# A four-layer network on one core: the step size dt as ln(1 + exp(x)), one half of the channels per round, without a lent PSUM bank and with fewer zero matmuls

## The chip, the cores and the metric

The kernel runs on one core of a Trainium2 chip. The time is the device time of that core in microseconds, the median of several runs. The profile is one execution of the program, taken on the chip. The engines are called TensorE (PE in the profile), VectorE (DVE), ScalarE (ACT) and GpSimd (POOL); SyncE (SP) issues the transfers.

## The reference

The network has four layers on four images of 56 x 56 tokens with 96 channels. Layers 2 and 3 are attention without a softmax and a quantised feed-forward part. Layers 0 and 1 each hold a selective scan over four orders of the tokens, and the scan takes most of the time. Cut to what matters:

```python
def selective_ssm(dtw, dtb, xw, A_log, D, seq):      # seq: images, 3136 tokens, 192 channels
    xz = jnp.einsum('bld,kd->blk', seq, xw)
    dt_raw, b_ssm, c_ssm = ...                       # 12 or 6, 16 and 16 columns of xz
    dt = jax.nn.softplus(jnp.einsum('blr,dr->bld', dt_raw, dtw) + dtb)
    a = -jnp.exp(A_log)
    d_a = jnp.exp(dt[..., None] * a)                 # the decays
    d_b = dt[..., None] * b_ssm[:, :, None, :]
    def step(h, inp):
        da_t, db_t, x_t, c_t = inp
        h = da_t * h + db_t * x_t[..., None]         # 192 x 16 states
        y_t = jnp.einsum('bds,bs->bd', h, c_t)
        return (h, y_t)
    ...
    return ys + seq * D
```

The softplus of x is ln(1 + exp(x)).

## The kernel before

The scan is cut into chunks of 448 tokens: 2 layers, 4 images, 4 orders and 7 chunks make 224. A chunk has 8 rounds, r = 0 to 7: two halves of 96 channels (e) times four groups of states (q). A round works on three tiles (g) of 128 rows by 448 tokens. For each, ScalarE makes the decay exp(dt * a) into one PSUM tile `da`, which the next round uses again; VectorE (or GpSimd for one of the three) multiplies dt * u with the B of the states, which TensorE has spread over the rows into one PSUM bank `b`; VectorE scans; GpSimd multiplies the states with C (`hc`); TensorE adds up over the states into the bank `y`, two rounds later, and after the fourth group ScalarE copies the sums to `Y`. While a chunk is scanned, the step sizes dt of the next are prepared. Beside the scan run lanes of side work, the other parts of the network for other images; they share two PSUM banks `ps` and are let in by an estimate of what ScalarE and TensorE have left.

Constants of the pacing:

```python
SPARE = (1.2, 3.0)
ACT_LIMIT, PE_LIMIT = 4.3, 6.0
SOFTPLUS = 2
BANKS, LATE_BANKS = 2, 4
DEPTH, LATE_DEPTH = 3, 6


WARM, FILL, PER_P = 1.9, 0.19, 0.58
```

The step sizes: the matmul for one half of the channels, the one made ahead in a lent bank, and the Softplus of both halves:

```python
    def step_sizes(self, ch):

        nc = self.nc
        ch.cd = self.dram.tile([2 * NS, CS], F32, tag="cd", name="cd", bufs=3)
        nc.sync.dma_start(ch.cd, ch.cf[: 2 * NS])
        ch.pd = [self.step_size(ch, 0, self.pp())]

    def step_size(self, ch, e, ps):
        rows = slice(32, 32 + RANK[ch.l])
        self.nc.tensor.matmul(ps[:C], ch.par.wt[rows, C * e : C * e + C], ch.cf[rows], start=True, stop=True)
        return ps[:C]

    def step_size_ahead(self, ch):

        if self.held < BANKS:
            ch.pd.append(self.step_size(ch, 1, self.ps()[:, :CS]))

    def softplus(self, ch):
        for e in range(NE):
            if e == len(ch.pd):
                ch.pd.append(self.step_size(ch, e, self.pp()))
            dt = self.sp.tile([C, CS], F32, name="dtc")
            self.nc.scalar.activation(dt, ch.pd[e], AF.Softplus, bias=ch.par.dtb[:, e : e + 1])
            ch.dtc.append(dt)
```

What is done for the following chunk in each round r of this one:

```python
        elif r == 1:
            self.step_sizes(follow)
            self.split(follow, 0)
        elif r == 2:
            self.softplus(follow)
            self.split(follow, 1)
        elif r == 3:
            self.times_u(follow, 0)
            for e in range(NE):
                self.park(follow.dtd, follow.dtc[e])
        elif r == 4:
            self.times_u(follow, 1)
            self.park(follow.dud, follow.duc[0])
            self.spread(follow.dt, follow.dtd[0], "dt")
        elif r == 5:
            self.park(follow.dud, follow.duc[1])
            self.spread(follow.du, follow.dud[0], "du")
        if r > 4:
            self.fetch(follow, r - 5)
```

The decay, and the loop over rounds (`begin` makes the spread of B on TensorE and, in most rounds, one of the three products on GpSimd; the yields let the side work, called lanes, put in its instructions):

```python
        def decay(n, g):

            ch, e, q = rounds[n]
            nc.scalar.activation(da[g][:, TOKENS], ch.dt[e][:, g], AF.Exp, scale=ch.par.na[:, e, q, g : g + 1])
# ... cut ...
            b, v, ahead = nxt
            for g in range(2 if ahead else 3):
                nc.vector.tensor_tensor(v[:, g, TOKENS], ch.du[e][:, g], b, ALU.mult)
            self.prepare(ch, nexts.get(ch), r)
            self.half_round()
            self.spend((0.6, 0, 3.8, 0, 0, 0, 0, 0)[r], (0, 1.3, 0, 0, 0, 0, 1.3, 1.3)[r] + 1.3 * (r % NQ == 2))
            self.limit = ACT_LIMIT if r >= SOFTPLUS else 0.5 + 0.95 * 2 * (SOFTPLUS - r)
            yield "C", n, r
            more = n + 1 < len(rounds)
            if more:
                nxt = begin(n + 1)
            ended = None
            if len(late) == 2:
                ended = late.pop(0)
                self.add_up(*ended)
            self.prepare_ahead(afters.get(ch), r)
            for g in range(NG):
                if g == 2:
                    self.half_round()
                    if ended and ended[2] == NQ - 1:
                        self.spend(0.6, 0)
                        self.keep_sums(*ended[:3])
                    if r < SOFTPLUS:
                        self.limit -= 0.95
                    yield "F", n, r
                    if r == 1 and ch in nexts:
                        self.step_size_ahead(nexts[ch])
                nc.vector.tensor_tensor_scan(
                    v[:, g, way], da[g][:, way], v[:, g, way], 0.0, ALU.mult, ALU.add
                )
                if g == 2 and ch.step < NCS - 1:
                    nc.scalar.copy(ch.par.carry[:, e, q].unsqueeze(2), v[:, :, end : end + 1])
                if more:
                    decay(n + 1, g)
                    if g == 0:
                        carried(n + 1, nxt[1])
            hc = sp.tile([128, NG, CS], F32, name="hc", bufs=3)
            nc.gpsimd.tensor_tensor(hc, v[:, :, TOKENS], ch.cb[q][:, 0].unsqueeze(1).to_broadcast([128, NG, CS]), ALU.mult)
            late.append((ch, e, q, hc))
```

Adding up, with its zero matmuls, and the copy of the sums:

```python
        for _ in range(int(max(0.0, WARM - self.work) / FILL + 0.5)):
            nc.tensor.matmul(self.y[:C], self.zeros, self.some, start=False, stop=False)
        self.work = 0.0

        for n, g in enumerate((0, 1, 2, 2)):
            nc.tensor.matmul(
                self.y[32 * n : 32 * n + 32], self.four, hc[:, g], start=n == 3, stop=n == 3 or q == NQ - 1,
            )

    def keep_sums(self, ch, e, q):

        y = self.in_order(self.Y[e], ch.orient, ch.c * CS, CS)
        self.nc.scalar.copy(y, self.y[:C].rearrange("p (a b) -> p a b", b=HS))
```

How a part of the side work is let in: its place names a slot and the banks it holds, and what it costs ScalarE (a) and TensorE (p):

```python
                held = sum(h[2] for h in self.live) - g[2] + new
                fits = held <= self.banks - self.lend or new <= g[2] and held <= self.banks
                if place[0] == self.slot and fits and self.room(act, pe):
                    self.spend(act, pe)
                    g[1], g[2] = next(g[0], None), new
# ... cut ...
    def spend(self, act, pe):
        self.work += PER_P * pe
        self.backlog = [a + b for a, b in zip(self.backlog, (act, pe))]

    def half_round(self):

        self.backlog = [max(0.0, a - b) for a, b in zip(self.backlog, SPARE)]

    def room(self, act, pe):

        a, p = self.backlog
        return not self.paced or (act == 0 or a + act <= self.limit) and (pe == 0 or p + pe <= PE_LIMIT)
```

The call:

```python
        for slot, n, r in net.scans():
            p, u = divmod(n, rounds)
            net.slot, net.lend, net.paced = slot, int(r < 2), True
```

The engines take their instructions in the order of the program. In `spend` the pacing counts what a part will cost; `half_round` takes off what an engine has spare in half a round; `room` refuses a part over the limit.

Of the kernel before, what the change touches and what calls it, by code (L numbers as in the profile page):

```python
# [11 lines left out]
F32 = mybir.dt.float32  # L12
# [8 lines left out]
HS = 56  # L21
L = HS * HS
C = 96
DI = 192
NS = 16
NE = 2
# [16 lines left out]
ACT_LIMIT, PE_LIMIT = 4.3, 6.0  # L43
SOFTPLUS = 2
BANKS, LATE_BANKS = 2, 4
# [118 lines left out]
class Net:  # L164
    def __init__(self, ctx, tc, aps, at, out):
# [5 lines left out]
        self.dram = pool("dram", bufs=1, space=bass.MemoryType.DRAM)  # L171
        self.nw, self.depth, self.banks, self.ring = NW, DEPTH, BANKS, None
        self.setup()
        self.dg = None
        self.kept = (0, 0, 0)
        self.ready = set()
        self.held, self.lend, self.live, self.g = 0, 0, [], {}
        self.backlog, self.limit, self.paced = [0.0, 0.0], ACT_LIMIT, False
        self.work = 0.0
# [10 lines left out]
    def late(self):  # L190

        self.scan_pool.close()
        self.wp = self.pool("late", bufs=2)
        self.nw, self.depth, self.banks = LATE_NW, LATE_DEPTH, LATE_BANKS
        tags = (("ps", BANKS), ("da0", 1), ("da1", 1), ("da2", 1), ("pp", 1), ("b", 1), ("y", 1))
        self.ring = cycle([t for t in tags for _ in range(t[1])])
# [284 lines left out]

    def step_size_ahead(self, ch):

        if self.held < BANKS:
            ch.pd.append(self.step_size(ch, 1, self.ps()[:, :CS]))

    def softplus(self, ch):
        for e in range(NE):
            if e == len(ch.pd):
                ch.pd.append(self.step_size(ch, e, self.pp()))  # L490
            dt = self.sp.tile([C, CS], F32, name="dtc")
            self.nc.scalar.activation(dt, ch.pd[e], AF.Softplus, bias=ch.par.dtb[:, e : e + 1])  # L492
            ch.dtc.append(dt)

# [31 lines left out]
    def prepare(self, ch, follow, r):  # L526
# [7 lines left out]
        if r == 0:  # L534
            self.rows(follow)
        elif r == 1:
            self.step_sizes(follow)
            self.split(follow, 0)
        elif r == 2:
            self.softplus(follow)  # L540
            self.split(follow, 1)
        elif r == 3:
            self.times_u(follow, 0)
            for e in range(NE):
                self.park(follow.dtd, follow.dtc[e])
        elif r == 4:
            self.times_u(follow, 1)
            self.park(follow.dud, follow.duc[0])
            self.spread(follow.dt, follow.dtd[0], "dt")
        elif r == 5:  # L550
            self.park(follow.dud, follow.duc[1])
            self.spread(follow.du, follow.dud[0], "du")
# [31 lines left out]
    def scans(self):  # L584
# [23 lines left out]
        first, second = chunks[:2]  # L608
        self.held = 0
        self.parameters(first)  # L610
# [3 lines left out]
        for r in range(8):  # L614
            self.prepare(Step(), first, r) if r else self.rows(first)
        self.parameters(second)
        self.project_step(second, 0)
# [34 lines left out]
        for n, (ch, e, q) in enumerate(rounds):  # L652
# [8 lines left out]
            self.half_round()  # L661
            self.spend((0.6, 0, 3.8, 0, 0, 0, 0, 0)[r], (0, 1.3, 0, 0, 0, 0, 1.3, 1.3)[r] + 1.3 * (r % NQ == 2))
            self.limit = ACT_LIMIT if r >= SOFTPLUS else 0.5 + 0.95 * 2 * (SOFTPLUS - r)
            yield "C", n, r
# [8 lines left out]
# [3 lines that stand above are left out]
                    if ended and ended[2] == NQ - 1:  # L676
                        self.spend(0.6, 0)
                        self.keep_sums(*ended[:3])
                    if r < SOFTPLUS:
                        self.limit -= 0.95  # L680
                    yield "F", n, r
                    if r == 1 and ch in nexts:
                        self.step_size_ahead(nexts[ch])
                nc.vector.tensor_tensor_scan(  # L684
# [16 lines left out]
    def add_up(self, ch, e, q, hc):  # L701

        nc = self.nc
        if q == 0:
# [3 lines left out]
            nc.tensor.matmul(o, w, self.in_order(a, ch.orient, ch.c * CS, CS), start=True, stop=False)  # L708
        for _ in range(int(max(0.0, WARM - self.work) / FILL + 0.5)):
            nc.tensor.matmul(self.y[:C], self.zeros, self.some, start=False, stop=False)  # L710
# [137 lines left out]
    def window(self, d, rows, c):  # L848

        lo, hi = max(0, CR * c - 1), min(HS, CR * c + CR + 1)  # L850
        t = self.wp.tile([128, CR + 2, HS], F32, name="win", bufs=NWIN)[:rows]
        self.nc.sync.dma_start(
# [4 lines left out]
    def overlap(self, part, n, depth=9, ready=lambda c: True):  # L857
# [5 lines left out]
        while live or c < n:  # L863
# [4 lines left out]
            for g in list(live):  # L868
# [4 lines left out]
                held = sum(h[2] for h in self.live) - g[2] + new  # L873
                fits = held <= self.banks - self.lend or new <= g[2] and held <= self.banks
                if place[0] == self.slot and fits and self.room(act, pe):
                    self.spend(act, pe)
                    g[1], g[2] = next(g[0], None), new
                    if g[1] is None:
                        live.remove(g)
                        self.live.remove(g)  # L880
            self.held = sum(h[2] for h in self.live)
            yield
# [9 lines left out]
    def room(self, act, pe):  # L892

        a, p = self.backlog
        return not self.paced or (act == 0 or a + act <= self.limit) and (pe == 0 or p + pe <= PE_LIMIT)

# [334 lines left out]
def tile_net(ctx: ExitStack, tc: tile.TileContext, aps, at, out):  # L1231
# [5 lines left out]
    def alone(lanes):  # L1237
        net.slot, net.lend, net.paced = "C", 0, False
        while lanes:
# [11 lines left out]
    with tc.manual_schedule(engines={E.PE, E.Activation, E.DVE, E.Pool}):  # L1251
        lanes = []
        for slot, n, r in net.scans():
            p, u = divmod(n, rounds)
            net.slot, net.lend, net.paced = slot, int(r < 2), True
            if slot == "C" and u == 2 and p < 8:
# [29 lines left out]
```

## Time and profile before

| | |
|---|---|
| time, median of 3 runs | 9214.4 us (9179.29 to 9226.93) |
| span of the profiled execution | 9209.2 us |
| mean granted clock of TensorE | 0.887 of full |
| from the first scan on (before: setup) | 111.4 us |
| end of the last scan (after: a tail of side work) | 8836.3 us |
| busy in the loop of scans, TensorE, VectorE, ScalarE, GpSimd | 7480.0, 7809.6, 5945.8, 7759.8 us |
| table loads on ScalarE in the program | 776 |
| zero matmuls | 7084 |

The page lists groups of instructions by line of the kernel, engine, operation and tiles (out<-in), with their count, busy time, the mean of one in ns, and after the bar the idle time of the engine just before them with what ended it. A line of the waits reads: who waited, for whom, us in total, times, longest. A line of the timeline reads: start in us, duration, engine, line, operation, tiles, count, and in brackets idle time before it and what ended that. L684 is the scan, L659 VectorE's products, L631 the decays, L646 and L688 the copies of the state carried from chunk to chunk, L492 the Softplus, L569 the spread of B, L694 the product with C, L710 the zero matmuls, L714 the adding up, L721 the copy of the sums, L479 the matmul of the step sizes.

### The profile page before, as it was taken

What the parts mean: (1) busy time and instruction counts of PE and PEld (TensorE: products, weight loads), DVE (VectorE), ACT (ScalarE), POOL (GpSimd) and SP (SyncE); (2) the same over time, 40 slices, a digit from 0 to 9 for tenths busy, and PEclk for the clock granted to TensorE, in tenths of its full rate; (3) what the DMA queues carried; (4) which work ended last, traced back from release to release, by engine and by line L of the source; (5) the groups of instructions that cost most, each with busy time, mean ns of one, the idle gap of its engine ahead of it and who ended that gap; (6) DMA issues with size and microseconds to landing.
All of it is one profiled execution on the core that took longest, in us unless ns stands there. A gap on an engine that the chain in (4) does not pass through costs nothing. (4 is left out here: it accounts for less than half of the span.)

```text
span 9209.2 us, 124390 instructions
## 1 busy us (share of the span) xinstructions
PE 7868.1 (85%) x35426; PEld 3036.5 (33%) x35426; DVE 7881.9 (86%) x10198; ACT 6148.3 (67%) x12259; POOL 7838.3 (85%) x4320
## 2 busy tenths in 40 slices
PE   7888888898888888988889888887888888987897
PEld 3333333333333333333333333333333333333344
DVE  5999999899998999989988997899888898888941
ACT  5777677676777677766776655577656776566645
POOL 5998989989898989889888997899888998888941
PEclk9899989989899988999888998888888888887986
DMA  5776676667666676767666775566755567655721
GB/s 151 176 179 169 166 171 164 157 153 177 162 168 157 157 181 161 169 150 177 162 148 152 168 170 136 136 153 160 171 138 143 141 164 172 147 138 134 168 77 39
DMA packets 951352, 1418.11 MB, mean 154 GB/s; under 512 B 176578, under 2 KB 943812, under 8 KB 949796
## 3 DMA queue, kind: packets, MB, share of 16 engines
q1 hardware_dynamic: 949888, 1408.37, 63.5%
q8 instruction: 278, 4.55, 0.2%
q14 instruction: 414, 3.39, 0.1%
q10 hardware_dynamic: 772, 1.80, 0.1%
HBM read 1141.42 MB, written 268.14 MB: 153 GB/s over the span
## 5 line engine op out<-in xcount | busy, mean ns | idle before, releaser
L684 DVE TENSOR_TENSOR_SCAN v<-da,v 128x449 f32<-128x449 f32 (+1 forms) x5376 | 5484.4, 1072 | 244.6 <-ACT da L631 111.0
L694 POOL TENSOR_TENSOR hc<-v,cb 128x1344 f32<-128x1344 f32 x1792 | 5168.0, 2885 | 573.5 <-DVE v L684 257.2
L631 ACT ACTIVATE da<-dt,na 128x448 f32<-128x448 f32 x5376 | 3392.8, 635 | 1690.3 <-DVE v L684 1650.9
L659 DVE TENSOR_TENSOR v<-du,b 128x448 f32<-128x448 f32 x4172 | 2342.3, 609 | 663.0 <-PE b L569 532.4
L714 PE MATMUL y<-hc,four 128*32 128x448 f32 x14336 | 1913.8, 609 | 0.0
L710 PE MATMUL y<-w,zeros 128*96 128x448 bf16 x7084 | 1716.6, 380 | 0.0
L639 POOL TENSOR_TENSOR v<-du,cb 128x448 f32<-128x448 f32 x1204 | 1373.7, 1141 | 79.0 <-DMA cb<-cd 41.6
L710 PEld LDWEIGHTS <-zeros 128*96 128x96 bf16 x7084 | 918.5, 130 | 1049.4 <-issue 639.9
L569 PE MATMUL b<-cf,sel 128*128 128x448 bf16 x1792 | 708.3, 395 | 350.9 <-DVE v L659 350.1
L761 POOL TENSOR_TENSOR rs<-rs,power 112x4 f32<-112x4 f32 x252 | 254.2, 1010 | 546.9 <-ACT rs L760 361.6
L427 PE MATMUL pp<-U,wd 96*128 96x448 f32 x896 | 674.5, 840 | 14.3 <-DMA U<-u 14.3
L721 ACT COPY Y<-y 96x448 f32<-96x448 f32 x448 | 341.3, 762 | 468.8 <-PE y L714 468.4
L841 PE MATMUL ps<-win,dg 64*64 64x220 f32 (+10 forms) x1962 | 568.4, 491 | 55.3 <-ACT dtc L492 47.0
L714 PEld LDWEIGHTS y<-hc,four 128*32 128x32 f32 x14336 | 295.3, 113 | 951.0 <-issue 649.1
L498 POOL TENSOR_TENSOR duc<-dtc,U 96x448 f32<-96x448 f32 x448 | 559.6, 1249 | 2.5 <-ACT dtc L492 2.5
L708 PE MATMUL y<-Y,ident 96*96 96x448 f32 x672 | 543.4, 898 | 11.4 <-ACT carry L688 8.9
L631 ACT ACT_TABLE_LOAD x385 | 494.0, 1283 | 15.1 <-DMA dt<-dd 8.3
L582 POOL TENSOR_TENSOR cf<-cf 64x448 f32<-64x448 f32 x448 | 417.7, 932 | 38.1 <-ACT cf L466 3.0
L569 PEld LDWEIGHTS <-sel 128*128 128x128 bf16 x1792 | 195.4, 109 | 741.4 <-issue 737.9
L688 ACT COPY carry<-v 128x3 f32<-128x3 f32 x1536 | 295.7, 193 | 172.1 <-DVE v L684 169.6
L765 PE MATMUL ps<-ident,rs 112*96 112x112 f32 x1752 | 267.7, 308 | 158.3 <-POOL rs L761 87.7
L841 PEld LDWEIGHTS ps<-win,dg 64*64 64x64 f32 (+2 forms) x1962 | 236.8, 169 | 423.7 <-issue 317.2
(414 smaller groups left out, 6457.5 us busy)
## 6 DMA issues: line engine op xcount, KB each, us to landing
cb<-cd SPq DMA_DIRECT2D x3584, 112.0 KB, 4.1
dt<-dd SPq DMA_DIRECT2D x1792, 168.0 KB, 4.4
du<-dd SPq DMA_DIRECT2D x1792, 168.0 KB, 4.2
dd<-dtc SPq DMA_DIRECT2D x448, 168.0 KB, 2.0
dd<-duc SPq DMA_DIRECT2D x448, 168.0 KB, 2.0
U<-u SPq DMA_DIRECT2D x112, 168.0 KB, 4.5
z<-w SPq DMA_DIRECT2D x56, 224.0 KB, 3.8
u<-w SPq DMA_DIRECT2D x56, 224.0 KB, 3.2
```

The costliest lines, as they stand in the source:

```text
L427: self.nc.tensor.matmul(ch.ps.rearrange("p (a b) -> p a b", b=HS), ch.par.wx[:, e], self.in_order(self.U[e], ch.orient, ch.c * CS, CS), st ...
L498: self.nc.gpsimd.tensor_tensor(du.rearrange("p (a b) -> p a b", b=HS), ch.dtc[e].rearrange("p (a b) -> p a b", b=HS), self.in_order(self.U ...
L569: self.nc.tensor.matmul(ps, self.sel[:, q], self.upper(ch.cf), start=True, stop=True)
L631: nc.scalar.activation(da[g][:, TOKENS], ch.dt[e][:, g], AF.Exp, scale=ch.par.na[:, e, q, g : g + 1])
L639: nc.gpsimd.tensor_tensor(v[:, 2, TOKENS], ch.du[e][:, 2], ch.cb[q][:, 1], ALU.mult)
L659: nc.vector.tensor_tensor(v[:, g, TOKENS], ch.du[e][:, g], b, ALU.mult)
L684: nc.vector.tensor_tensor_scan(v[:, g, way], da[g][:, way], v[:, g, way], 0.0, ALU.mult, ALU.add)
L694: nc.gpsimd.tensor_tensor(hc, v[:, :, TOKENS], ch.cb[q][:, 0].unsqueeze(1).to_broadcast([128, NG, CS]), ALU.mult)
L708: nc.tensor.matmul(o, w, self.in_order(a, ch.orient, ch.c * CS, CS), start=True, stop=False)
L710: nc.tensor.matmul(self.y[:C], self.zeros, self.some, start=False, stop=False)
L714: nc.tensor.matmul(self.y[32 * n : 32 * n + 32], self.four, hc[:, g], start=n == 3, stop=n == 3 or q == NQ - 1,)
L841: self.nc.tensor.matmul(o[:, a - r0 : e - r0, x0:x1], diag[:, tap], win[:, a + dy - lo : e + dy - lo, x0 + dx : x1 + dx], start=n == 0, st ...
```

## The change

It writes softplus as two activations, Exp and then Ln of it plus one, so that ScalarE may do it with the tables that the decays use. It does one half of the channels in round 2 and the other in round 3, so that the second half needs no bank of its own: its matmul goes to `pp` after the first half has been read, and the `ps` bank that was lent to it stays with the side work. The limit that held side work back on ScalarE ahead of the Softplus goes; each of the two rounds is charged 1.3 us. The zero matmuls, which keep TensorE at work before an adding up, are left out where the sums are copied right after it. In the part after the scans, windows get as many buffers as there are parts under way (6 for 3). All of it is here:

```diff
--- before.py
+++ after.py
@@ -41,7 +41,6 @@
 
 SPARE = (1.2, 3.0)
 ACT_LIMIT, PE_LIMIT = 4.3, 6.0
-SOFTPLUS = 2
 BANKS, LATE_BANKS = 2, 4
 DEPTH, LATE_DEPTH = 3, 6
 
@@ -169,13 +168,13 @@
         self.big = pool("big", bufs=1)
         self.psum = pool("psum", bufs=1, space=bass.MemoryType.PSUM)
         self.dram = pool("dram", bufs=1, space=bass.MemoryType.DRAM)
-        self.nw, self.depth, self.banks, self.ring = NW, DEPTH, BANKS, None
+        self.nw, self.nwin, self.depth, self.banks, self.ring = NW, NWIN, DEPTH, BANKS, None
         self.setup()
         self.dg = None
         self.kept = (0, 0, 0)
         self.ready = set()
-        self.held, self.lend, self.live, self.g = 0, 0, [], {}
-        self.backlog, self.limit, self.paced = [0.0, 0.0], ACT_LIMIT, False
+        self.live, self.g = [], {}
+        self.backlog, self.paced = [0.0, 0.0], False
         self.work = 0.0
         self.U = [self.big.tile([C, L], F32, name=f"U{e}") for e in range(NE)]
         self.Y = [self.big.tile([C, L], F32, name=f"Y{e}") for e in range(NE)]
@@ -191,7 +190,7 @@
 
         self.scan_pool.close()
         self.wp = self.pool("late", bufs=2)
-        self.nw, self.depth, self.banks = LATE_NW, LATE_DEPTH, LATE_BANKS
+        self.nw, self.nwin, self.depth, self.banks = LATE_NW, LATE_DEPTH, LATE_DEPTH, LATE_BANKS
         tags = (("ps", BANKS), ("da0", 1), ("da1", 1), ("da2", 1), ("pp", 1), ("b", 1), ("y", 1))
         self.ring = cycle([t for t in tags for _ in range(t[1])])
 
@@ -479,18 +478,15 @@
         self.nc.tensor.matmul(ps[:C], ch.par.wt[rows, C * e : C * e + C], ch.cf[rows], start=True, stop=True)
         return ps[:C]
 
-    def step_size_ahead(self, ch):
-
-        if self.held < BANKS:
-            ch.pd.append(self.step_size(ch, 1, self.ps()[:, :CS]))
-
-    def softplus(self, ch):
-        for e in range(NE):
-            if e == len(ch.pd):
-                ch.pd.append(self.step_size(ch, e, self.pp()))
-            dt = self.sp.tile([C, CS], F32, name="dtc")
-            self.nc.scalar.activation(dt, ch.pd[e], AF.Softplus, bias=ch.par.dtb[:, e : e + 1])
-            ch.dtc.append(dt)
+    def softplus(self, ch, e):
+
+
+
+
+        dt = self.sp.tile([C, CS], F32, name="dtc")
+        self.nc.scalar.activation(dt, ch.pd[e], AF.Exp, bias=ch.par.dtb[:, e : e + 1])
+        self.nc.scalar.activation(dt, dt, AF.Ln, bias=1.0)
+        ch.dtc.append(dt)
 
     def times_u(self, ch, e):
 
@@ -537,14 +533,15 @@
             self.step_sizes(follow)
             self.split(follow, 0)
         elif r == 2:
-            self.softplus(follow)
+            self.softplus(follow, 0)
             self.split(follow, 1)
         elif r == 3:
+            self.softplus(follow, 1)
             self.times_u(follow, 0)
-            for e in range(NE):
-                self.park(follow.dtd, follow.dtc[e])
+            self.park(follow.dtd, follow.dtc[0])
         elif r == 4:
             self.times_u(follow, 1)
+            self.park(follow.dtd, follow.dtc[1])
             self.park(follow.dud, follow.duc[0])
             self.spread(follow.dt, follow.dtd[0], "dt")
         elif r == 5:
@@ -606,13 +603,14 @@
                             setattr(ch, n_, [])
                         chunks.append(ch)
         first, second = chunks[:2]
-        self.held = 0
         self.parameters(first)
         self.inputs(first)
         self.project_step(first, 0)
         self.project_step(first, 1)
         for r in range(8):
             self.prepare(Step(), first, r) if r else self.rows(first)
+            if r == 2:
+                first.pd.append(self.step_size(first, 1, self.pp()))
         self.parameters(second)
         self.project_step(second, 0)
         self.project_step(second, 1)
@@ -659,8 +657,7 @@
                 nc.vector.tensor_tensor(v[:, g, TOKENS], ch.du[e][:, g], b, ALU.mult)
             self.prepare(ch, nexts.get(ch), r)
             self.half_round()
-            self.spend((0.6, 0, 3.8, 0, 0, 0, 0, 0)[r], (0, 1.3, 0, 0, 0, 0, 1.3, 1.3)[r] + 1.3 * (r % NQ == 2))
-            self.limit = ACT_LIMIT if r >= SOFTPLUS else 0.5 + 0.95 * 2 * (SOFTPLUS - r)
+            self.spend((0.7, 0, 1.3, 1.3, 0, 0, 0, 0)[r], (0, 1.3, 1.3, 0, 0, 0, 1.3, 1.3)[r] + 1.3 * (r % NQ == 2))
             yield "C", n, r
             more = n + 1 < len(rounds)
             if more:
@@ -676,11 +673,9 @@
                     if ended and ended[2] == NQ - 1:
                         self.spend(0.6, 0)
                         self.keep_sums(*ended[:3])
-                    if r < SOFTPLUS:
-                        self.limit -= 0.95
                     yield "F", n, r
-                    if r == 1 and ch in nexts:
-                        self.step_size_ahead(nexts[ch])
+                    if r == 2 and ch in nexts:
+                        nexts[ch].pd.append(self.step_size(nexts[ch], 1, self.pp()))
                 nc.vector.tensor_tensor_scan(
                     v[:, g, way], da[g][:, way], v[:, g, way], 0.0, ALU.mult, ALU.add
                 )
@@ -706,7 +701,7 @@
             o = self.y[:C].rearrange("p (a b) -> p a b", b=HS)
             a, w = (self.U[e], self.skip[ch.l][:, e]) if ch.skip else (self.Y[e], self.ident[:C, :C])
             nc.tensor.matmul(o, w, self.in_order(a, ch.orient, ch.c * CS, CS), start=True, stop=False)
-        for _ in range(int(max(0.0, WARM - self.work) / FILL + 0.5)):
+        for _ in range(int(max(0.0, WARM - self.work) / FILL + 0.5) if q < NQ - 1 else 0):
             nc.tensor.matmul(self.y[:C], self.zeros, self.some, start=False, stop=False)
         self.work = 0.0
 
@@ -848,7 +843,7 @@
     def window(self, d, rows, c):
 
         lo, hi = max(0, CR * c - 1), min(HS, CR * c + CR + 1)
-        t = self.wp.tile([128, CR + 2, HS], F32, name="win", bufs=NWIN)[:rows]
+        t = self.wp.tile([128, CR + 2, HS], F32, name="win", bufs=self.nwin)[:rows]
         self.nc.sync.dma_start(
             t[:, : hi - lo].rearrange("p a b -> p (a b)"), d[:, lo * HS : hi * HS]
         )
@@ -871,14 +866,12 @@
                 times = {t[0]: float(t[1:]) for t in times}
                 act, pe = times.get("a", 0.0), times.get("p", 0.0)
                 held = sum(h[2] for h in self.live) - g[2] + new
-                fits = held <= self.banks - self.lend or new <= g[2] and held <= self.banks
-                if place[0] == self.slot and fits and self.room(act, pe):
+                if place[0] == self.slot and held <= self.banks and self.room(act, pe):
                     self.spend(act, pe)
                     g[1], g[2] = next(g[0], None), new
                     if g[1] is None:
                         live.remove(g)
                         self.live.remove(g)
-            self.held = sum(h[2] for h in self.live)
             yield
 
     def spend(self, act, pe):
@@ -892,7 +885,7 @@
     def room(self, act, pe):
 
         a, p = self.backlog
-        return not self.paced or (act == 0 or a + act <= self.limit) and (pe == 0 or p + pe <= PE_LIMIT)
+        return not self.paced or (act == 0 or a + act <= ACT_LIMIT) and (pe == 0 or p + pe <= PE_LIMIT)
 
 
     def load(self, i):
@@ -1235,7 +1228,7 @@
         return [lane for lane in lanes if next(lane, lane) is not lane]
 
     def alone(lanes):
-        net.slot, net.lend, net.paced = "C", 0, False
+        net.slot, net.paced = "C", False
         while lanes:
             lanes = go_on(lanes)
             net.slot = "CF"[net.slot == "C"]
@@ -1252,7 +1245,7 @@
         lanes = []
         for slot, n, r in net.scans():
             p, u = divmod(n, rounds)
-            net.slot, net.lend, net.paced = slot, int(r < 2), True
+            net.slot, net.paced = slot, True
             if slot == "C" and u == 2 and p < 8:
 
                 assert p > 5 or not lanes
```

## The prediction

> **What bounds the kernel now.** I read the page's busy times first, then the groups, the waits, and last a timeline of one chunk. The loop of scans runs from 111.4 to 8836.3 us (starts and ends of L684 in the trace), 95% of the span, so its 224 chunks of 8 rounds are what counts.
>
> ```profile
> PE 7868.1 (85%) x35426; PEld 3036.5 (33%) x35426; DVE 7881.9 (86%) x10198; ACT 6148.3 (67%) x12259; POOL 7838.3 (85%) x4320
> ```
>
> Three engines are near 85%, none at 100%. By its busy time VectorE is the first: its scans and products have to be done in any case. So the question is what ends its idle time. From the groups and the waits:
>
> ```profile
> L684 DVE TENSOR_TENSOR_SCAN v<-da,v 128x449 f32<-128x449 f32 (+1 forms) x5376 | 5484.4, 1072 | 244.6 <-ACT da L631 111.0
> L659 DVE TENSOR_TENSOR v<-du,b 128x448 f32<-128x448 f32 x4172 | 2342.3, 609 | 663.0 <-PE b L569 532.4
> ACT da L631 <- DVE v L684: 1650.9, 2126, 6.3
> DVE v L659 <- PE b L569: 532.4, 369, 6.5
> ACT Y L721 <- PE y L714: 468.4, 337, 9.2
> DVE v L684 <- ACT da L631: 111.0, 118, 2.5
>   PEld ps L841: 62.5, 21
>   PE ps L765: 54.7, 22
> ```
>
> ScalarE waits 1651 us for scans, VectorE only 111 us for decays: today ScalarE runs ahead. VectorE's largest wait is for TensorE's spread of B (`b`), 532 us. The last two lines are from the answer on L492, of who waited for the step sizes `dtc`: side work that needs a `ps` bank waits until the Softplus has read the one lent to it, and TensorE, which takes its matmuls in order, keeps `b` back meanwhile.
>
> I then sorted VectorE's idle time by round r of the chunk (each scan triple is one round). A chunk takes 38.96 us, 4.08 of it idle; before round 3 alone it is 1.57, of which 1.24 is the wait for `b`. 49 chunks have no side work (under 0.7 us of ScalarE outside the scan's own lines): 35.8 us each, idle before round 3 0.94, all of it ScalarE's. The 175 others: 39.8 us, idle before round 3 1.75, 1.59 of it for `b`. A quiet chunk, ScalarE and then VectorE around rounds 2 to 4:
>
> ```profile
> 4114.09 1.00 ACT L721 COPY Y<-y 96x448 f32<-96x448 f32 x1 [1.00 <-PE y L714]
> 4114.94 0.63 ACT L631 ACTIVATE da<-dt,na 128x448 f32<-128x448 f32 x1
> 4115.60 1.28 ACT L492 ACT_TABLE_LOAD   x1
> 4116.89 0.63 ACT L492 ACTIVATE dtc<-pp,wd 96x448 f32<-96x448 f32 x1
> 4117.42 0.62 ACT L492 ACTIVATE dtc<-ps,wd 96x448 f32<-96x448 f32 x1
> 4118.06 1.28 ACT L631 ACT_TABLE_LOAD   x1
> 4119.35 0.64 ACT L631 ACTIVATE da<-dt,na 128x448 f32<-128x448 f32 x1
> 4125.81 0.64 ACT L631 ACTIVATE da<-dt,na 128x448 f32<-128x448 f32 x1 [1.84 <-DVE v L684]
> 4129.82 0.64 ACT L631 ACTIVATE da<-dt,na 128x448 f32<-128x448 f32 x1 [1.31 <-DVE v L684]
> 4117.32 1.65 DVE L659 TENSOR_TENSOR v<-du,b 128x448 f32<-128x448 f32 x3
> 4120.14 3.06 DVE L684 TENSOR_TENSOR_SCAN v<-da,v 128x449 f32<-128x449 f32 x3 [1.16 <-ACT v L646]
> ```
>
> The Softplus block runs from 4115.60 to 4119.35, 3.75 us, of which 2.57 are two table loads; VectorE's scans of round 3 stall 1.16 us behind it.
>
> **The arithmetic of a block.** In undisturbed rounds a decay ends 2.3 us before its scan starts (medians of the trace), 2.8 us where VectorE makes three products, as before rounds 3 and 4. That is the slack. Ahead of a round's first decay ScalarE idles 1.31 us (after two products) or 1.84 us (after three), as the brackets above show. So a block of B us makes the decays B minus that idle late, plus what was late already, and VectorE stalls by the lateness over the slack. Tried on the chunk above: the copy of `Y` had made round 2's last decay 1.4 late; 3.75 + 1.4 - 1.31 = 3.84, less 2.8 gives 1.04 against 1.16 seen.
>
> [...]
>
> **The change, part by part.**
>
> 1. **Softplus becomes Exp and Ln.** The text means to save both loads. I choose to doubt that. [...] Nothing in the changed kernel names another set. Then each Ln needs a load, and unless that load fetches the joint set, the next decay needs one back. Two halves, two Ln: 4 loads a chunk where there were 2. Each half then is 0.63 (Exp) + 1.28 + 0.63 (Ln) + 1.28 = 3.82 us, with joints 3.85: a Softplus block of the old length, twice, in rounds 2 and 3. On ScalarE: 224 x about 3.9 = 870 us more busy, to about 7000. I give the joint set one chance in ten.
>
> 2. **No bank lent.** The second step size goes to `pp` after the first Exp has read it. TensorE's waits for `dtc` (about 480 us in the ten largest of that answer, TensorE and its weight loads) should nearly go, and with them most of the 1.59 before round 3 in busy chunks: I take 1.3 off. Side work may hold both banks in rounds 0 and 1.
>
> 3. **The pacing.** Side work on ScalarE was held back over rounds 0 and 1 to make room; now it is not, and rounds 2 and 3 are charged 1.3 us each for what I expect to be 3.85. Busy chunks have 6.7 us of side work on ScalarE, 0.83 a round, and now it also falls into these rounds.
>
> 4. **No zeros ahead of the sums that are copied at once.** The trace has 5.1 zero matmuls ahead of an add-up with q=3 of the first half and 3.6 of the second, some 1950 of 7084; at 0.21 us from one to the next about 410 us of TensorE. TensorE isn't the bound there, but the `Y` copy waits for these sums (468 us), and it stands ahead of decays. In the quiet chunk six zeros took 1.35 us just ahead. So the decay after the copy should be 0.5 late, not 1.4.
>
> Sum for a **quiet** chunk: round 3: late 3.85 + 0.5 - 1.31 = 3.04, stall 0.3. Behind a stall the first decay is late by the slack, and each further one gains about 0.35, as a scan takes 1.02 and a decay with its copies less; so the third is about 2.1 late. Round 4: 2.1 + 3.85 - 1.84 = 4.1, stall 1.3, with the carry's copy 1.45. Together 1.75, against 1.2 now: +0.5, times 49 is +25 us.
>
> A **busy** chunk: with 0.83 of side work in each: round 3 stalls 1.2, round 4 2.1 + 0.83 + 3.85 - 1.84 = 4.94, so 2.2. Together 3.4. Off go 1.3 (the wait for `b`), 0.4 (other idle before round 4, 0.56 now, which hides under the stall) and 0.15 (the ScalarE stall of now before round 3): +1.55, times 175 is +271 us.
>
> Credits: the stall before round 6 behind the `Y` copy, 0.30 in busy chunks, nearly goes: -44. Side work that moves in rounds 0 and 1: I estimate -40. The tail of 373 us gets six window buffers for three: at most -5. Sum 9214 + 25 + 271 - 89 = about **9420 us**.
>
> **The rivals.** (a) The joint set is loaded[...]: no load but side work's, each half 1.26 us, no stall in rounds 3 and 4. Then 1.2 is saved in quiet and about 1.75 in busy chunks: 49 x 1.2 + 175 x 1.75 + 89 = 454, so near 8760 us. For it speaks the name of the change[...]. (b) Four loads, but the bound is the bank: side work in the small rounds is little (0.51, 0.07 and 0.32 us in rounds 0 to 2 now) and stays so; the stalls are those of quiet chunks and freeing the bank pays for them: near 9150. (c) TensorE takes the place of the bank: side work's `ps` tiles now wait for evictions that stand behind two blocks in ScalarE's queue, `b` comes late at rounds 3 and 4 both, and 0.8 us more a busy chunk: near 9560. (d) Fewer zeros lower the granted clock. The zeros' share of TensorE falls by 410 us only, and other matmuls stand next to them; I give it 30 us at most.
>
> **The range.** (a) has 0.1. For four loads my sum lies between (b) and (c), and its largest term, the two stalls in busy chunks, is uncertain by some 1 us a chunk or 175 us. So 9190 to 9650 should hold it 8 times in 10. The lines at 2% are 9030 and 9399: faster 0.10, same 0.35, slower 0.55.
>
> **What would show it.** Table loads: 776 now, about 1220 with four a chunk, about 330 with the joint set. VectorE's wait for decays and carries rises from some 180 us to 500 or more, and stands before rounds 3 and 4; its wait for `b` falls by 200 or more; waits of TensorE for `dtc` nearly vanish; the wait of the `Y` copy falls by about half. I am wrong if the loads don't rise, if the wait for `b` stays, or if the stalls before round 4 are under 1 us.

## The result, and the profile after

The changed kernel takes 9510 us (9484 to 9522, four runs) where the kernel before takes 9211 in the runs beside it: 1.0325 times as long, 95% interval 1.0289 to 1.0361. Every ratio below is likewise against runs of the kernel before that were taken beside it (medians of 9198 to 9211 us). The page of the changed kernel: first busy times, then groups (after the bar the idle time ahead of the group and what ended most of it).

```profile
PE 7874.2 (83%) x33219; PEld 2896.8 (30%) x33219; DVE 7906.5 (83%) x10198; ACT 6929.2 (73%) x13156; POOL 7834.7 (82%) x4320
...
L679 DVE TENSOR_TENSOR_SCAN v<-da,v 128x449 f32<-128x449 f32 (+1 forms) x5376 | 5485.6, 1072 | 538.4 <-ACT v L644 346.9
...
L657 DVE TENSOR_TENSOR v<-du,b 128x448 f32<-128x448 f32 x4172 | 2341.0, 608 | 682.5 <-PE b L566 554.1
...
L629 ACT ACT_TABLE_LOAD x608 | 780.1, 1283 | 19.2 <-DMA dt<-dd 8.5
...
L488 ACT ACT_TABLE_LOAD x448 | 574.8, 1283 | 7.9
```

The loads of the kernel before at the decays (L631) and at the Softplus (L492):

```profile
L631 ACT ACT_TABLE_LOAD x385 | 494.0, 1283 | 15.1 <-DMA dt<-dd 8.3
...
L492 ACT ACT_TABLE_LOAD x224 | 287.4, 1283 | 4.0
```

Of the waits, first four of the changed kernel and then the one of the kernel before for the copy of the carry, L646:

```profile
DVE v L657 <- PE b L566: 554.1, 393, 5.9
...
DVE v L679 <- ACT v L644: 346.9, 327, 3.4
...
ACT Y L716 <- PE y L709: 310.6, 192, 5.3
...
DVE v L679 <- ACT da L629: 133.2, 142, 3.3
```

```profile
DVE v L684 <- ACT v L646: 70.2, 75, 2.6
```

The lines have moved: L679 is the scan, L657 the products, L629 the decays, L487 the Exp and L488 the Ln of the step size, L644 and L683 the copies of the carry, L566 the spread of B, L709 the adding up, L716 the copy of the sums. VectorE does the same work (scans 5486 us, 5484 before) and waits longer: for decays and carries 480 us (346.9 and 133.2), where it was 181 (111.0 and 70.2). ScalarE has 781 us more to do: 449 more table loads (1225, 776 before) at 1283 ns are 576 us of it. Every one of the 448 Ln has a load ahead of it, and L629, the decays, has 608 for 385. So Exp and Ln did not share their tables.

A quiet chunk of the changed kernel, from the load behind the Ln of round 2 to the decay behind the Ln of round 3, and VectorE beside it (start, duration, engine, line, operation; in brackets idle time and what ended it):

```profile
3275.77 1.28 ACT L629 ACT_TABLE_LOAD   x1
3277.07 0.64 ACT L629 ACTIVATE da<-dt,na 128x448 f32<-128x448 f32 x1
...
3278.95 0.62 ACT L487 ACTIVATE dtc<-pp,wd 96x448 f32<-96x448 f32 x1
3279.59 1.28 ACT L488 ACT_TABLE_LOAD   x1
3280.88 0.58 ACT L488 ACTIVATE dtc<-dtc 96x448 f32<-96x448 f32 x1
3281.47 1.28 ACT L629 ACT_TABLE_LOAD   x1
3282.77 0.64 ACT L629 ACTIVATE da<-dt,na 128x448 f32<-128x448 f32 x1
```

```profile
3277.86 3.06 DVE L679 TENSOR_TENSOR_SCAN v<-da,v 128x449 f32<-128x449 f32 x3 [0.74 <-ACT v L644]
3280.83 1.66 DVE L657 TENSOR_TENSOR v<-du,b 128x448 f32<-128x448 f32 x3
3283.56 3.06 DVE L679 TENSOR_TENSOR_SCAN v<-da,v 128x449 f32<-128x449 f32 x3 [1.07 <-ACT v L644]
```

The block of round 3, from its Exp to the next decay, runs from 3278.95 to 3282.77, 3.82 us. VectorE stalls in two rounds, 0.74 and 1.07 us, where in the quiet chunk shown of the kernel before it stalled 1.16 in one.

All kernels side by side, VectorE's idle time ahead of each round, in us per chunk, summed from each run's trace (the mean of 224 chunks). The times are medians; the trace of "both Ln in round 3" is of an execution of 9211 us:

| kernel | 0 | 1 | 2 | 3 | 4 | 5 | 6 | 7 | sum | time |
|---|---|---|---|---|---|---|---|---|---|---|
| before | 0.59 | 0.30 | 0.24 | 1.57 | 0.44 | 0.28 | 0.43 | 0.23 | 4.08 | 9211 |
| after | 0.72 | 0.60 | 0.52 | 0.83 | 1.54 | 0.76 | 0.32 | 0.17 | 5.46 | 9510 |
| joint set | 0.87 | 0.59 | 0.58 | 0.15 | 0.42 | 0.30 | 0.26 | 0.17 | 3.34 | 8981 |
| joint set, one bank in rounds 0, 1 | 0.73 | 0.33 | 0.26 | 0.20 | 0.60 | 0.31 | 0.29 | 0.19 | 2.91 | 8916 |
| before with the joint set | 0.58 | 0.26 | 0.33 | 0.71 | 0.55 | 0.26 | 0.60 | 0.26 | 3.55 | 9078 |
| both Ln in round 3 | 0.80 | 0.61 | 0.35 | 0.15 | 1.39 | 0.29 | 0.28 | 0.25 | 4.12 | 9239 |
| second half in round 4 | 0.60 | 0.64 | 0.57 | 0.89 | 0.68 | 0.41 | 0.52 | 0.30 | 4.61 | 9322 |

The table says where the 299 us are: rounds 3 to 5, where the blocks are, went from 2.29 to 3.13, and rounds 0 to 2 from 1.13 to 1.84. In the two profiled executions the loop of scans takes 334 us more (9059 for 8725) and the tail behind it 29 less (344 for 373).

### The profile page after: what moved, and what is told of

Its sections match the earlier page's. It is cut to its first block, busy times and chain, and to the rows that moved or that the text cites. A ratio compares the mean times of both kernels' runs of the same rounds, so it can differ in the third digit from the quotient of the medians.

```text
span 9517.1 us, 120632 instructions
## 1 busy us (share of the span) xinstructions
PE 7874.2 (83%) x33219; PEld 2896.8 (30%) x33219; DVE 7906.5 (83%) x10198; ACT 6929.2 (73%) x13156; POOL 7834.7 (82%) x4320
## 5 line engine op out<-in xcount | busy, mean ns | idle before, releaser
L679 DVE TENSOR_TENSOR_SCAN v<-da,v 128x449 f32<-128x449 f32 (+1 forms) x5376 | 5485.6, 1072 | 538.4 <-ACT v L644 346.9
L629 ACT ACTIVATE da<-dt,na 128x448 f32<-128x448 f32 x5376 | 3386.3, 635 | 1262.1 <-DVE v L679 1202.0
L657 DVE TENSOR_TENSOR v<-du,b 128x448 f32<-128x448 f32 x4172 | 2341.0, 608 | 682.5 <-PE b L566 554.1
L709 PE MATMUL y<-hc,four 128*32 128x448 f32 x14336 | 2059.1, 652 | 1.0 <-POOL hc L689 0.9
L566 PE MATMUL b<-cf,sel 128*128 128x448 bf16 x1792 | 744.9, 416 | 702.7 <-DVE v L657 701.0
L705 PE MATMUL y<-w,zeros 128*96 128x448 bf16 x4877 | 1323.0, 412 | 0.0
L705 PEld LDWEIGHTS <-zeros 128*96 128x96 bf16 x4877 | 688.5, 141 | 875.5 <-issue 643.2
L629 ACT ACT_TABLE_LOAD x608 | 780.1, 1283 | 19.2 <-DMA dt<-dd 8.5
L709 PEld LDWEIGHTS y<-hc,four 128*32 128x32 f32 x14336 | 304.5, 117 | 1080.2 <-issue 760.5
L488 ACT ACT_TABLE_LOAD x448 | 574.8, 1283 | 7.9
L716 ACT COPY Y<-y 96x448 f32<-96x448 f32 x448 | 339.7, 758 | 312.6 <-PE y L709 310.6
L478 PE MATMUL pp<-cf,wd 12*96 12x448 f32 (+1 forms) x896 | 510.3, 653 | 1.1 <-ACT cf L465 0.8
L760 PE MATMUL ps<-ident,rs 112*96 112x112 f32 x1800 | 286.8, 316 | 198.2 <-POOL rs L756 179.9
L566 PEld LDWEIGHTS <-sel 128*128 128x128 bf16 x1792 | 197.6, 110 | 792.8 <-issue 789.1
```

The costliest lines, as they stand in the source:

```text
L488: self.nc.scalar.activation(dt, dt, AF.Ln, bias=1.0)
L566: self.nc.tensor.matmul(ps, self.sel[:, q], self.upper(ch.cf), start=True, stop=True)
L679: nc.vector.tensor_tensor_scan(v[:, g, way], da[g][:, way], v[:, g, way], 0.0, ALU.mult, ALU.add)
L709: nc.tensor.matmul(self.y[32 * n : 32 * n + 32], self.four, hc[:, g], start=n == 3, stop=n == 3 or q == NQ - 1,)
```

## The experiments

Two causes stood against each other. Theory A: the loads. Theory B: the zeros left out, since the mean granted clock fell from 0.887 to 0.825 and the mean of an adding-up matmul rose from 609 to 652 ns.

### The joint set by name

The joint set of the prediction is the one that this edit loads:

```diff
+    def tables(self, joint):
+        if joint and not self.joint:
+            self.nc.scalar.preload_act_table_set("natural_log_exp_and_others")
+        self.joint = joint
# ... cut ...
     # self.tables(True) ahead of decays, of the Exp of the step size and of na;
     # self.tables(False) ahead of each Silu and Gelu; once more set to False in round 2 of the loop
```

> The changed kernel with the joint set of exp and ln loaded by name after each use of another set, so that Exp and Ln take no load: about 334 loads in the program for 1225. Theory A (the loads cost it): VectorE's wait for decays and carries (480 us now, 181 before) falls to about 150, the time to about 9180 us. Theory B (the zeros left out cost it, by a lower granted clock: 0.825 after, 0.887 before): the clock stays near 0.825, the wait for B (554 us) stays, and the time stays above 9400 us.

Measured: 8981 us, 0.976 of before (0.9733 to 0.9788), with 334 loads. From the groups on ScalarE and the waits (who, for whom: us, times, longest), where L200 is the loading of the joint set, L690 the scan, L668 the products, L638 the decays:

```profile
L200 ACT ACT_TABLE_LOAD x163 | 209.1, 1283 | 2.9
...
L495 ACT ACT_TABLE_LOAD x2 | 2.6, 1283 | 0.0
L496 ACT ACT_TABLE_LOAD x2 | 2.6, 1283 | 0.0
```

```profile
DVE v L668 <- PE b L574: 480.5, 379, 5.7
...
DVE v L690 <- ACT da L638: 56.5, 57, 2.4
```

Exp (L495) and Ln (L496), 448 of each, take four loads in the whole program. The two activations, the split over two rounds, the bank and the zeros are all as in the change; only the loads are gone, and with them 529 us. (The pacing's charge of 1.3 us a round, too low before, now fits a block without loads; what the charge alone does is shown below.) The clock was still low, 0.856. That fits theory A in kind, and the gain is far over what it gave (9180 expected): the waits for decays and carries fell to 77 us, but the stalls that the loads make are not only those. Ahead of round 5 the wait for B alone went from 0.53 to 0.19 us a chunk.

### The zeros back

```diff
-        for _ in range(int(max(0.0, WARM - self.work) / FILL + 0.5) if q < NQ - 1 else 0):
+        for _ in range(int(max(0.0, WARM - self.work) / FILL + 0.5)):
```

> The changed kernel with the zeros back ahead of the sums copied at once; its four loads a chunk stay. Theory A: 9470 to 9530 us, the stalls behind the loads as after. Theory B: the clock comes back to about 0.88, the wait for B falls from 554 to 350 us or less, and the time to about 9250 us.

Measured: 9549 us, 1.039 of before (1.0359 to 1.0422), clock 0.867. With more clock it is 39 us slower than the change, 19 over what theory A gave, and the wait for B hardly moved (543 us for 554). Theory B falls.

The same line put back on the kernel with the joint set:

> Both: the joint set and the zeros back. If the two effects add up: theory A about 9150 us, little under the joint set alone; theory B about 8950 us, some 200 us under the joint set alone, with the clock at 0.88.

Measured: 8978 us, 0.9763 (0.974 to 0.9787), clock 0.891. The time is near theory B's number, but for another reason: the joint set alone already had it. 0.856 or 0.891 of the clock made no difference there.

And the zeros left out of the kernel before, nothing else:

```diff
-        for _ in range(int(max(0.0, WARM - self.work) / FILL + 0.5)):
+        for _ in range(int(max(0.0, WARM - self.work) / FILL + 0.5) if q < NQ - 1 else 0):
```

> The kernel before with one part of the change alone: no zeros ahead of the sums copied at once. Theory A: the copy of Y waits less (468 us before), the time 9170 to 9220 us. Theory B: the clock falls to about 0.83, matmuls and the wait for B (532 us) grow, and the time is 9350 us or more.

Measured: 9141 us, 0.9932 (0.9912 to 0.9952), clock 0.85. The waits of this run:

```profile
DVE v L659 <- PE b L569: 557.7, 375, 5.6
...
ACT Y L721 <- PE y L714: 263.6, 207, 7.4
```

The copy of the sums waits 264 us for 468, and the kernel gains 61 us, a little more than either theory gave it. So this part of the change helps, at a lower clock; the wait for B rose by 25 us only.

### What holds B back in rounds 0 to 2

With the joint set the stall ahead of round 3 is gone (1.57 to 0.15), but rounds 0 to 2 wait 0.91 us a chunk longer than before. Theory C blames the second bank that side work may now use in rounds 0 and 1; theory D the hold-back of side work on ScalarE that went with the lent bank.

```diff
-                if place[0] == self.slot and held <= self.banks and self.room(act, pe):
+                if place[0] == self.slot and (held <= self.banks - self.keep or new <= g[2] and held <= self.banks) and self.room(act, pe):
# ... cut ...
-            net.slot, net.paced = slot, True
+            net.slot, net.keep, net.paced = slot, int(r < 2), True
```

> The joint set, with the side work held to one ps bank in rounds 0 and 1 as before the change, though nothing is lent. With the joint set VectorE waits 1.52 us a chunk for B ahead of rounds 0 to 2, where the kernel before waits 0.75. Theory C (the freed bank lets side matmuls in ahead of B): those waits fall back to about 0.8 and the time from 8981 to about 8830 us. Theory D (it is the hold-back of side work on ScalarE that went): no change, 8960 to 9000 us.

Measured: 8916 us, 0.9691 (0.9659 to 0.9723), the fastest of all; VectorE idles 1.32 us ahead of rounds 0 to 2 for 2.04, of which the wait for B is 0.90 for 1.51. The waits, lines as in the run with the joint set:

```profile
DVE v L668 <- PE b L574: 370.5, 292, 5.5
```

The wait fell nearly as far as theory C said (0.8), the time by 65 us of the 150. In the profiled executions the loop of scans is 109 us shorter (8440 for 8549), and the tail behind it 44 us longer (365 for 321): side work that was held back is done after the scans, where ScalarE has 357 instructions for 322.

The hold-back instead of the bank:

```diff
+            self.limit = ACT_LIMIT if r >= 2 else 0.5 + 0.95 * 2 * (2 - r)
# ... cut ...
+                    if r < 2:
+                        self.limit -= 0.95
# ... cut ...
-        return not self.paced or (act == 0 or a + act <= ACT_LIMIT) and (pe == 0 or p + pe <= PE_LIMIT)
+        return not self.paced or (act == 0 or a + act <= self.limit) and (pe == 0 or p + pe <= PE_LIMIT)
```

> The joint set, with the hold-back of side work on ScalarE over rounds 0 and 1 put back as before the change. Theory C: no change, 8960 to 9000 us. Theory D: the waits for B ahead of rounds 0 to 2 fall from 1.52 us a chunk to about 0.8, the time to about 8830 us.

Measured: 8995 us, 0.9776 (0.9745 to 0.9806): no gain on the 8981 of the joint set. VectorE idles 2.07 us ahead of rounds 0 to 2, and its wait for B there rose from 1.51 to 1.75. Theory C holds, at half the gain in time, and D falls. With one bank round 0 still waits 0.73. One bank in round 7 too, where the B of round 0 is spread:

```diff
-            net.slot, net.keep, net.paced = slot, int(r < 2), True
+            net.slot, net.keep, net.paced = slot, int(r < 2 or r == 7), True
```

> The joint set with side work held to one bank in rounds 7, 0 and 1. With one bank in rounds 0 and 1 VectorE still waits 0.63 us a chunk for B ahead of round 0, which is spread in round 7. If side matmuls with two banks in round 7 make it, it falls to about 0.3 and the time from 8916 to about 8850 us; if side work only moves to other rounds, the time stays within 20 us.

Measured: 8948 us, 0.9729 (0.9706 to 0.9752). Round 0 waits 0.52 instead of 0.73 and round 4 0.77 instead of 0.60: the side work moves, and 32 us are lost; the tail grew too (385 us for 365).

### How a load costs

```diff
-        self.nc.scalar.activation(dt, dt, AF.Ln, bias=1.0)
         ch.dtc.append(dt)
+        if e == NE - 1:
+            for dt in ch.dtc:
+                self.nc.scalar.activation(dt, dt, AF.Ln, bias=1.0)
-            self.spend((0.7, 0, 1.3, 1.3, 0, 0, 0, 0)[r], ...)
+            self.spend((0.7, 0, 0.7, 4.5, 0, 0, 0, 0)[r], ...)
```

> The changed kernel with no set named, but with both Ln in a row in round 3 behind the second Exp: two loads a chunk for four (777 in all), one block of about 4.4 us in round 3. If the cost goes with the loads and with blocks standing one behind the other, the stall ahead of round 3 (0.83 us a chunk) goes, that ahead of round 4 (1.54) stays at 1.0 to 1.5, and the time is about 9200 us, 300 under the change. If any load costs its own 1.28 us of path and no more, the two loads saved are worth 1.28 x 2 x 224 = 570 us: 8940 us.

Measured: 9239 us over twenty runs, 1.0043 (1.0031 to 1.0054). Half the added loads are gone, and half of the 529 us (271), where a fixed 1.28 us a load would give 570. The stall ahead of round 3 went to 0.15, that ahead of round 4 stayed at 1.39. The run also charges its block in round 3 nearly what it takes (4.5 us), so the 271 us hold a part that is not the loads'; the run with the charge alone, below, gains 88.

```diff
         elif r == 3:
-            self.softplus(follow, 1)
             self.times_u(follow, 0)
             self.park(follow.dtd, follow.dtc[0])
         elif r == 4:
-            self.times_u(follow, 1)
-            self.park(follow.dtd, follow.dtc[1])
+            self.softplus(follow, 1)
             self.park(follow.dud, follow.duc[0])
             self.spread(follow.dt, follow.dtd[0], "dt")
         elif r == 5:
+            self.times_u(follow, 1)
+            self.park(follow.dtd, follow.dtc[1])
+            self.spread(follow.du, follow.dud[0], "du")
+        elif r == 6:
             self.park(follow.dud, follow.duc[1])
-            self.spread(follow.du, follow.dud[0], "du")
# ... cut ...
-            self.spend((0.7, 0, 1.3, 1.3, 0, 0, 0, 0)[r], ...)
+            self.spend((0.7, 0, 1.3, 0, 1.3, 0, 0, 0)[r], ...)
```

> The changed kernel, four loads a chunk, with the second half moved from round 3 to round 4, so that a round without a block lies between. By the arithmetic of lateness over slack: ahead of round 5 the decays are 3.85 + 0.8 (side work) - 1.84 = 2.8 late against a slack of 2.3, a stall of 0.5 where the second block now stalls 0.97 ahead of round 4; with the rest of the lateness gone about 0.7 us a chunk less, about 9350 us. If a load costs its own time wherever it stands, no change: 9510.

Measured: 9322 us, 1.0136 (1.0111 to 1.0161). As many loads as the change (1225 in the program), 188 us less: ahead of rounds 4 and 5 VectorE idles 1.09 us for 2.30. So a load has no fixed cost here: it depends on where its block stands. The arithmetic of lateness over slack came near in the time, but not in its parts: the stall behind ScalarE ahead of round 5 is 0.16 us, not 0.5, and ahead of round 3 it stayed (0.77 for 0.68).

```diff
-            self.spend((0.7, 0, 1.3, 1.3, 0, 0, 0, 0)[r], ...)
+            self.spend((0.7, 0, 3.8, 3.8, 0, 0, 0, 0)[r], ...)
```

> The changed kernel, four loads, with rounds 2 and 3 charged 3.8 us each for 1.3. If the wrong charge is what makes busy chunks stall, the waits for decays and carries (480 us) fall to about 350 and the time by 50 to 120 us, to about 9420 us. If the two blocks alone do it, side work or not, the time stays within 30 us of 9510.

Measured: 9422 us, 1.0235 (1.0208 to 1.0262), 88 us under the change; the waits for decays and carries fell to 406 us and the idle time ahead of round 5 from 0.76 to 0.03 us a chunk. So the wrong charge was a part of the loss, 88 of 299 us, and the larger one stays with the blocks charged rightly. In the loop of scans alone the charge counts for more: the loop takes 8891 us in the profiled execution, 166 more than before the change, where the change has 334 more. But side work that is held back is done in the tail, which grew (422 us for 344).

### The tables without the rest

```diff
-            self.nc.scalar.activation(dt, ch.pd[e], AF.Softplus, bias=ch.par.dtb[:, e : e + 1])
+            self.tables(True)
+            self.nc.scalar.activation(dt, ch.pd[e], AF.Exp, bias=ch.par.dtb[:, e : e + 1])
+            self.nc.scalar.activation(dt, dt, AF.Ln, bias=1.0)
-            self.spend((0.6, 0, 3.8, 0, 0, 0, 0, 0)[r], ...)
+            self.spend((0.6, 0, 2.6, 0, 0, 0, 0, 0)[r], ...)
```

The set is named in the same places as in the first experiment.

> The kernel before with Exp and Ln from the joint set in place of the Softplus, both halves in round 2, the bank still lent and the zeros as before. It tells what the tables bring without the rest of the change. If the lent bank is what holds B back (1.24 us a chunk ahead of round 3), that wait shrinks only with the block, from 3.75 to about 2.5 us, and the time is about 9050 us, over the 8916 us of the joint set with nothing lent. If the loads alone made that wait, it goes, and the time is 8900 to 8950 us.

Measured: 9078 us, 0.9874 (0.9848 to 0.9901). The wait for B ahead of round 3 falls from 1.24 to 0.69 us and does not go: the loads lengthened it, and what is left goes only with the rest of the change (0.14 with the joint set there). The bank that is no longer lent is part of that rest; no run changes it alone. That rest is worth another 97 us on the joint set (9078 to 8981).

## Why the prediction was right, and where its sum was not

The time foretold was 9420 us in 9190 to 9650, with slower the likeliest; 9510 came. The mechanism held: four loads a chunk, two long blocks, longer stalls behind ScalarE ahead of rounds 3 and 4. That the sum came within 90 us is in part luck: in busy chunks two of its terms missed by about 1.7 us each, in opposite directions (item 3). Of the three signs of being wrong one came, as the wait for `b` stayed, and one nearly did: ScalarE's stall ahead of round 4 is 0.97 us (1.54 with every cause). The waits for decays and carries, put at 500 us or more, are 480.

1. **The loads** went as chosen: 1225 for about 1220; ScalarE 781 us more busy for 870, the Ln taking 0.58 us for 0.63. That each Ln would need a load, and the decay behind it another, was the author's estimate, and so was the one chance in ten for the joint set: the kernel before has no Ln, so no trace of it could show this. The changed kernel does: 448 loads for 448 Ln (L488), 608 for 385 at the decays (L629), and in the setup, where no decay stands between the two halves, Exp, Ln, Exp and Ln take a load each (at 79.16, 81.78, 83.66 and 85.61 us). Once the program loaded the joint set by name, the 896 Exp and Ln of the step sizes took four loads in all.

2. **The quiet chunk** is the term that came out best: 35.8 to 36.2 us, +0.4 for +0.5. The stalls were 0.66 and 0.98 in the mean for 0.3 and 1.45, 1.64 for 1.75 together. The +0.5 counted from the 1.2 of one chunk; from the mean of 0.94 the stalls rose by 0.7, and part of that is offset by less idle time ahead of round 0 (1.57 for 2.00), which was in no term. The decay behind the copy of `Y` was 1.2 late, not 0.5: the copy itself takes 1.0 us (1.00 at 4114.09 in the kernel before, 1.00 at 3271.82 in the changed one), which I had left out. ScalarE kept the order of the program there: in the kernel before, the scan that the decay needed had ended at 4113.38, and the decay started at 4114.94, behind the copy that had waited 1.00 us for its sums.

3. **The busy chunk** is where the sum failed, twice, in opposite directions: 39.8 to 42.0, +2.2 for +1.55. ScalarE's stalls ahead of rounds 3 and 4 were put at 3.4 us and are 1.66 (0.69 and 0.97); another 0.21 stands ahead of round 5. They are as long as in quiet chunks (0.66 and 0.98): the 0.83 us of side work that the sum added to each block does not show in them. Where it went is not shown; it may lie under the waits for B. And the credit of 1.3 for the freed bank was wrong: ahead of round 3 the wait for B did fall, from 1.59 to 0.19, but in the other rounds it rose from 1.4 to 3.2. This is rival (c) in part (round 5: 0.73, most of which goes without the loads, by the run with the joint set, and all idle time there but 0.03 with the right charge) and the freed bank itself in rounds 0 to 2 (by the run with one bank). The sign that B's wait falls by 200 us did not come: 554 us for 532. TensorE's waits for `dtc`, summed over all its instructions, did fall, from 597 to 107 us. How they kept B back shows in the kernel before at 1845.08: a matmul of side work (L841) has waited 4.72 us for `dtc`, the spread of B behind it starts at 1846.76, and VectorE has waited 1.88 us for that.

4. **The zeros**: 2207 fewer for about 1950. The copy's wait fell by a third (468 to 311), not by half. The clock fell from 0.887 to 0.825, and no run shows a cost of it: with the zeros back it is 0.867, and the change is slower by 39 us.

5. **Side work** did move on sooner: 163 busy chunks for 175. The tail behind the scans fell by 29 us, where at most 5 had been credited; no run tells the windows from the side work done sooner. Rival (a), the joint set, was put at 8760 and is 8981: the same wrong credit for the bank, as rounds 0 to 2 idle 0.91 us a chunk longer, 204 us in all. Rival (b), that the freed bank pays for the blocks, is ruled out: ahead of round 3 it did pay, but longer waits for B in the other rounds took that back.

## What to carry to other kernels

Exp and Ln shared their tables here only where the program loaded the joint set by name (334 loads for 1225), so count the table loads in the trace, and name the set if they are there. What a block of work cost on the engine that runs ahead depended here on where it stood: two blocks in neighbouring rounds took 188 us more than two with a round between, with the same 1225 loads. When a bank or a wait is freed, ask what else will use it: with side work free to use both banks VectorE waited 1.51 us a chunk for B ahead of rounds 0 to 2, with one bank in rounds 0 and 1 it waited 0.90. And where side work is held back, look at what it adds behind the loop: here it took back 44 of 109 us.

## What the runs showed that was not expected

The clock: five kernels with a mean granted clock of 0.85 to 0.86 (8916, 8948, 8981, 8995 and 9141 us) are faster than the kernel before at 0.887, and the three pairs that differ in the zeros alone show -61, -39 and +3 us for leaving them out. In each of the three pairs the zeros brought the higher granted clock (0.887 for 0.85, 0.867 for 0.825, 0.891 for 0.856), and they stand ahead of needed matmuls. And the 1.283 us that a table load takes were not what it cost: on the change 891 fewer loads gave 529 us, 0.59 us each, with the charge that then fits among it; on the kernel before 442 fewer, with the Softplus written as Exp and Ln, gave 121 us on the runs beside it, 0.27 each.
